# The maxima of the second attention go round three PSUM banks

## The chip, the cores and the metric

The kernel runs on one core of a Trainium2 chip. The metric is the device time of one execution in microseconds (us). Three runs of the kernel before took 4518.84, 4525.36 and 4537.07 us, a median of 4525.36. The profile is of one further execution.

## What is computed

The model is a chain of residual blocks over four sequences of 512 tokens and 128 channels: a gated mixture of experts, a linear attention, the experts again, a six-layer block of local attention and feed-forward (`_L1_ffn_ref`), the attention that this case is about (`_L1_attn_ref`), and the six-layer block once more.

```python
x = x + 0.5 * _L1_ffn_ref(_layernorm(x), ...)
x = x + _L1_attn_ref(_layernorm(x), ...)
x = x + 0.5 * _L1_ffn_ref(_layernorm(x), ...)
```

The second attention has 16 heads of 8 channels and two softmax branches, which share queries and values and differ in their keys:

```python
q, k, v, kp = (_heads(x @ W.T, B, T) for W in (W_Q, W_K, W_V, W_K_prime))
attn   = softmax(einsum('bhqd,bhkd->bhqk', q, k)  / sqrt(8))
attn_p = softmax(einsum('bhqd,bhkd->bhqk', q, kp) / sqrt(8))
out = alpha * (attn @ v) + (1 - alpha) * (attn_p @ v)
return out.transpose(0, 2, 1, 3).reshape(B, T, C) @ W_O.T
```

## The kernel before

The program has four parts, run one after the other: the front (experts and linear attention), the first six-layer block, the second attention (`l1_attn`, line 1061), the second six-layer block. In the six-layer blocks the order of work on every engine is written out by hand. In the second attention only TensorE's order is (`slots`, line 1271, under `manual_schedule` for PE); the order on the vector, scalar and GpSimd engines and on SP's DMA queue is chosen by a scheduler that simulates the program when it is built.

The attention's work is cut into 32 units (`todo`, line 1220): four sequences b, two branches br, four groups hg of four heads. Queries and keys are held as three bfloat16 pieces stacked along the contraction, 72 rows of products and zeros up to row 96; rows 96 to 98 of the keys hold ones and those of the queries take the negated row maxima, in three pieces as well. One matmul then yields score minus maximum.

A unit passes through these steps:

- `max` (line 1145), 16 times: one matmul S (L1147) of 128 queries against 512 keys into a PSUM bank, and one reduction on the vector engine, DVE (L1148), which writes the negated maximum into a column of `nm`.
- `pieces` (L1156 to L1160, GpSimd): the maxima are split into three pieces.
- `rows`: a transpose (nmT, L1165), a copy on ScalarE, ACT (npc, L1167), a DMA to DRAM (nd, L1169) and a DMA back into rows 96 to 98 of the queries (q<-nd, L1170). Both are issued on SP's queue.
- `score` (L1176, L1177), 16 times: the matmul ST, the other way round, into one of four banks with the tag `mm`, and an exponential on ACT.
- `mix` (L1184): E times the values and a column of ones, accumulated in the bank `av`.
- `norm` (L1194 to L1205): a transpose (avT, in an `mm` bank), a reciprocal, a scaling and a multiplication on DVE.

A unit is worked on over four slots. In slot n (`slot`, line 1236) the maxima of unit n, the rows of unit n-1, the scores and mixes of unit n-2 and the last mixes and the normalisation of unit n-3 share the engines. A slot has four blocks (kt = 0 to 3). In each block TensorE's order is S, ST, S, ST, S, ST, S, ST and then the mix of the block before. `rows` comes after the second pair of block 1, `norm` at the end of block 1, so that its transposes open block 2. In slots 0 and 1 there are maxima but no scores; in slots 32 to 34 there are scores but no maxima.

Between the units, in blocks 0 and 3, runs the preparation of the next sequence (`prep`, line 1100): a layer norm and its transpose (yT), three projections (qp, L274 to L276), each split into three pieces by ACT, DVE (L1114), ACT and GpSimd (L1116) and written to DRAM by three DMAs (pd, L1120), and the projection of the values (vp). `load` (line 1094) brings the queries and keys of the next sequence back from DRAM by four DMAs, one for each group of heads (q<-pd and k<-pd, L1098). When a sequence is done, `final` multiplies by W_O (OT, wop) and adds to x (L1217). All these DMAs go through SP's queue, which works in order.

PSUM has eight banks of 512 fp32 values in each partition. The pool (line 63) gives four to the tag `mm`, one to `n2`, two to `S` (its tile has 1024 values, line 69) and one to `av`. A call of `bank` allocates a tile; with one buffer to a tag, the new tile waits until the one before has been released, that is until its last reader is done.

In `max` the maxima alternate between the tags `S` and `n2`: for an even `qt` a new tile of `S` is allocated, of which the first 512 values are used, for an odd one a tile of `n2`. The second bank of `S` is not used in this stage. The six-layer blocks use `S` whole, for their scores, and `n2` for their norms.

Of the kernel before, what the change touches and what calls it, by code (L numbers as in the profile page):

```python
# [66 lines left out]

BANKS = {"mm": 4, "n2": 1, "S": 1, "av": 1}


def bank(g, tag, shape=(128, 512), name=None):
    n = math.prod(shape[1:])
    t = g.psum.tile([128, 1024 if tag == "S" else 512], F32, tag=tag, name=name or tag, bufs=BANKS[tag])[0:shape[0], 0:n]
    if len(shape) > 2:
        d = "abcd"[:len(shape) - 1]
        t = t.rearrange("p (%s) -> p %s" % (" ".join(d), " ".join(d)), **dict(zip(d[1:], shape[2:])))
    return t
# [201 lines left out]
class Unit:  # L279


    def __init__(self, g, l, hf, b):
        self.g, self.l, self.hf, self.b = g, l, hf, b
        self.raw, self.pt, self.v = [None, None], {}, [None, None]
        self.rt = [None, None]
        self.sqs, self.S = {}, {}

# [122 lines left out]
    def score(self, k, h):  # L410
# [3 lines left out]
        if h == 0:  # L414
            self.S[k] = S = bank(g, "S", [128, 2, 512])
            for p in range(4):
                for ab in range(2):
                    rows, q = slice(ab * 64, ab * 64 + 64), slice(p * 32, p * 32 + 32)
                    nc.tensor.matmul(S[q, ab].rearrange("p (a b) -> p a b", b=64) if k else S[q, ab], lhsT=g.msel[rows],
                                     rhs=g.mask1[rows].unsqueeze(1).to_broadcast([64, 8, 64]) if k  # L420
                                     else g.mask0[rows].rearrange("k a b c -> k (a b c)"), start=True, stop=False)
        for w in range(4 * h, 4 * h + 4):
            t0 = (8 * k + w) * 32
            n = 64 if t0 else 32
            for p in range(4):
                for ab in range(2):
                    rows = slice(ab * 64, ab * 64 + 64)
                    nc.tensor.matmul(self.S[k][p * 32:(p + 1) * 32, ab, w * 64 + 64 - n:w * 64 + 64],  # L428
                                     lhsT=self.rt[1][rows, p, t0:t0 + 32], rhs=self.rt[0][rows, p, t0 + 32 - n:t0 + 32],
# [631 lines left out]
def l1_attn(g, w, x, ev, t0=0.0, blk=0, ready=None, memory=()):  # L1061
# [32 lines left out]
    def load(b, i):  # L1094

        t = qs[b % 2] if i == 0 else ks[i - 1]
        for hg in range(4):
            nc.sync.dma_start(t[hg // 2][0:SR, hg % 2], dram[(b, i)][:, :, :, hg].rearrange("a c d h n -> (a c d) h n"))  # L1098

    def prep(b):  # L1100
        y = g.wp.tile([128, 4, 128], F32, tag="wvraw", name="y", bufs=1)
        layernorm(g, x[b], y)
        p = bank(g, "mm", name="yT")
        transpose4(g, p, y)
        xT = g.wp.tile([128, 2, 512], FR, tag="rot", name="xT", bufs=3)
        split(g, xT[:, 0, :], xT[:, 1, :], p)
        yield
        for i, n in enumerate(("W_Q", "W_K", "W_K_prime")):
            p = bank(g, "mm", name="qp")
            mm3(nc, p, W[n][:, 0, :], W[n][:, 1, :], xT[:, 0, :], xT[:, 1, :])  # L1110
            pc = tile_of(g, "pt", [128, 3, 512], BF, "pc")
            t1 = g.wp.tile([128, 512], F32, tag="woraw", name="t1", bufs=1)
            nc.scalar.copy(pc[:, 0, :], p)
            nc.vector.tensor_tensor(t1, p, pc[:, 0, :], ALU.subtract)  # L1114
            nc.scalar.copy(pc[:, 1, :], t1)
            (nc.gpsimd if b else nc.vector).tensor_tensor(pc[:, 2, :], t1, pc[:, 1, :], ALU.subtract)  # L1116
            dram[(b, i)] = d = g.dr.tile([3, 3, 8, 4, 4, 512], BF, tag="pd", name="pd", bufs=4)
            for c in range(3):
                dst = d[:, c] if i == 0 else d[c]
                nc.sync.dma_start(dst.rearrange("j d g h n -> (d g h) j n"), pc)  # L1120
            if i == 0 and b:
                load(b, i)
            yield
        p = bank(g, "mm", [128, 4, 16, 8], "vp")
        for t in range(4):
            ts = slice(t * 128, (t + 1) * 128)
            mm3(nc, p[:, t], xT[:, 0, ts], xT[:, 1, ts], W["W_V"][:, 0, :], W["W_V"][:, 1, :])
        if b == 0:
            vxs.extend(columns())
        vx = vxs[b % 2]  # L1130
        nc.vector.tensor_copy(vx[:, :, 0:144].rearrange("p t (h c) -> p t h c", c=9)[:, :, :, 0:8], p)
        st[b] = tile_of(g, "t2", [128, 4, 16, 8], name="O")
        yield

    class Unit1:
# [7 lines left out]
            self.nm = tile_of(g, "nm", [128, 4, 4], bufs=3)  # L1143

        def max(self, h, qt):
            S = bank(g, ("S", "n2")[qt % 2], name="S")
            nc.tensor.matmul(S, lhsT=self.q[0:R0, h, qt * 128:(qt + 1) * 128], rhs=self.k[0:R0, h, :], start=True, stop=True)  # L1147
            nc.vector.tensor_reduce(self.nm[:, h, qt:qt + 1], S, AX.X, ALU.max, negate=True)  # L1148

# [68 lines left out]
            yield  # L1218

    todo = [(b, br, hg) for b in range(4) for br in range(2) for hg in range(4)]  # L1220
    units = []
    extra = []

    def first():
# [8 lines left out]
    def pick(n):  # L1233
        return units[n] if 0 <= n < len(units) else None

    def slot(n):
        if n < len(todo):
            units.append(Unit1(*todo[n]))
            if n % 8 == 3 and n < 24:
                extra.append(prep(n // 8 + 1))  # L1240

        if n % 8 == 4 + LAG and n < 24:
            load(n // 8 + 1, 1)
        if n % 8 == LAG and 8 < n < 32:
            load(n // 8, 2)
        U, P, A, B = (pick(n - k) for k in (0, 1, LAG, LAG + 1))
        for kt in range(4):
            if (kt in (0, 3) or not A) and extra:
                if next(extra[0], 0) == 0:
                    extra.pop(0)  # L1250
            for h in range(4):
                if U:
                    U.max(kt, h)
                if A:
                    A.score(kt, h)
                if kt == 1 and h == 1 and P:
                    P.rows()
                if h == 3:
                    for c in range(2):
                        if kt and A:  # L1260
                            A.mix(kt - 1, c)
                        if kt == 0 and B:
                            B.mix(3, c)
            if kt == 1 and B:
                B.norm()
                if (B.br, B.hg) == (1, 3):
                    extra.insert(0, B.final())
            if U and kt == 3:
                U.pieces()

    def slots():
        for n in range(len(todo) + LAG + 2):
            with g.tc.manual_schedule(engines={mybir.EngineType.PE}):
                if n < len(todo) + LAG + 1:
                    slot(n)
                else:
                    for e in extra:
                        for _ in e:
                            pass
            yield  # L1280
# [18 lines left out]
def macaron(tc, w, out):  # L1299
    with ExitStack() as ctx:  # L1300
# [13 lines left out]
        def side():  # L1314
# [9 lines left out]
        l1_ffn(g, w, x, ev, xd=xd, ready=names[-4:])  # L1324
        ev.part = 2
        ready = l1_attn(g, w, x, ev, PHASES[0], ready=[((5, b), "fadd", 0) for b in range(4)],
                        memory=[((5, 1, 3), "vproj", 7, 1), ((5, 1, 3), "score", 1, 1, 0)])
        ev.part = 3
# [28 lines left out]
```

## Time and profile before

| | |
|---|---|
| median of three runs | 4525.36 us |
| the profiled execution: its time | 4526.41 us |
| its span, first to last instruction | 4524.2 us |
| busy in the span: PE, DVE, ACT, POOL | 86%, 82%, 58%, 55% |
| mean granted clock of PE | 0.94 |
| first and last reduction of the maxima (L1148) | 2306.5 and 2773.2 us |
| reductions L1148 | 512, 684 ns each |
| exponentials L1177 | 512, 597 ns each |

PE is TensorE's matmuls, PEld its weight loads, DVE the vector engine, ACT ScalarE, POOL GpSimd, and SPq the queue from which SP issues DMAs. Times in a timeline count from the start of the span. A line gives the start, the duration, the engine, the source line, the operation, what it writes and reads, how many instructions were merged into it, and in brackets the idle time before it with the instruction that ended it. Several matmuls overlap in TensorE, so the distance from start to start says more than the duration. The busy shares are means over the whole span; the second attention is about a tenth of it.

### The profile page before, as it was taken

The page shows a single profiled execution, that of the slowest core. Times are in us where ns is not written, and L with a number is a line of the kernel's source. Part 1 is how long each engine was busy: PE and PEld are TensorE (multiplying, and loading weights), DVE is VectorE, ACT ScalarE, POOL GpSimd, SP SyncE. Part 2 cuts the span into 40 slices and gives each one's busy share as a digit, 9 for nine tenths or more (in the row PEclk, how much of TensorE's full clock was granted, in tenths as well). Part 3 has the DMA queues.
Part 4 walks back from the last instruction along what each step waited for, and adds up shares of the span by engine and source line. Part 5 has one row for each costly group of instructions (what it writes and reads, how often), then busy time and mean ns, then how long its engine had stood idle before and what let it go on. Part 6 is the DMA issues. An engine that isn't in the chain of part 4 may idle for free.

```text
span 4524.2 us, 150230 instructions
## 1 busy us (share of the span) xinstructions
PE 3890.1 (86%) x66432; PEld 2671.8 (59%) x66436; DVE 3712.5 (82%) x6415; ACT 2622.0 (58%) x5050; POOL 2491.7 (55%) x2164
## 2 busy tenths in 40 slices
PE   8989978898888888898869998888889888888886
PEld 6666646666666666666523333666666666666654
DVE  6967978888888888988767775888888888888886
ACT  4534455665565565665546666556566556565653
POOL 3625656666666666666410111666666666666663
PEclk8989989999999999999979999999999999999998
DMA  2000033433424334343331221333343333333432
GB/s 61 19 10 15 19 85 74 91 70 80 91 61 91 70 80 90 64 90 73 82 102 35 68 73 35 83 69 81 77 92 70 79 79 75 82 69 79 86 62 48
DMA packets 163852, 312.44 MB, mean 69 GB/s; under 512 B 41304, under 2 KB 125664, under 8 KB 138176
## 3 DMA queue, kind: packets, MB, share of 16 engines
q0 software_dynamic: 31008, 202.40, 22.6%
q1 hardware_dynamic: 132192, 100.44, 7.6%
q8 instruction: 520, 8.52, 0.8%
q14 instruction: 132, 1.08, 0.1%
HBM read 77.49 MB, written 17.69 MB: 21 GB/s over the span
## 4 chain that ended last, share of the span: by engine, by line
DVE 41%; PE 36%; DMA 11%; issue 6%; ACT 3%; POOL 2%; SPq 0%; DVEq 0%; ACTq 0%; POOLq 0%
DMA xs<-x 9%; DVE sm L448 4%; DVE E L440 3%; DVE h L935 3%; PE vps L401 3%; PE S L428 3%; DVE mx L438 3%; DVE xT L269 3%; PE av L1184 3%; PE S L1147 3%; DVE pt L455 3%; DVE rtq L308 3%; PE av L471 2%; PE qkps L274 2%; DVE nm L1148 2%
## 5 line engine op out<-in xcount | busy, mean ns | idle before, releaser
L310 POOL TENSOR_TENSOR raw<-raw,rot 128x512 f32<-128x512 f32 x768 | 1007.1, 1363 | 540.1 <-ACT raw L300 536.5
L300 ACT COPY raw<-qkps 128x512 f32<-128x512 f32 x768 | 453.4, 590 | 654.3 <-PE qkps L276 636.6
L401 PE MATMUL vps<-vo,xF 128*32 128x256 f32 x12288 | 748.3, 386 | 35.6 <-issue 26.3
L401 PEld LDWEIGHTS vps<-vo,xF 128*32 128x32 f32 x12288 | 408.4, 111 | 321.3 <-issue 77.5
L452 POOL TENSOR_TENSOR E<-E,smr 128x1024 f32<-128x1024 f32 x192 | 389.5, 2028 | 310.5 <-DVE smr L450 161.5
L407 ACT COPY vx<-vps 128x512 f32<-128x512 f32 x768 | 426.9, 584 | 105.5 <-PE vps L401 103.3
L303 ACT ACTIVATE sq<-qkps 128x512 f32<-128x512 f32 x768 | 473.0, 616 | 0.0
L443 POOL TENSOR_TENSOR E<-E,rq 128x1024 f32<-128x1024 f32 x192 | 388.9, 2026 | 96.5 <-DVE E L440 57.6
L471 PE MATMUL av<-vx,pt 128*32 128x128 f32 x11904 | 382.0, 275 | 59.4 <-DVE x L478 33.2
L274 PE MATMUL qkps<-xT,wqk 128*128 128x512 f32 x768 | 344.9, 449 | 80.4 <-DVE rtq L308 42.1
L471 PEld LDWEIGHTS av<-vx,pt 128*32 128x32 f32 x11904 | 335.6, 110 | 117.4 <-DVE x L478 50.3
L1148 DVE TENSOR_REDUCE nm<-S 128x1 f32<-128x512 f32 x512 | 326.6, 684 | 81.6 <-PE S L1147 73.8
L308 DVE TENSOR_TENSOR rtq<-qkps,rot 128x512 f32<-128x512 f32 x384 | 259.9, 685 | 135.7 <-ACT sq L303 134.1
L1177 ACT ACTIVATE E<-ST 128x512 f32<-128x512 f32 x512 | 289.5, 597 | 116.3 <-PE ST L1176 105.6
L383 DVE TENSOR_TENSOR rtk<-rtk,R 128x512 f32<-128x512 f32 x384 | 254.1, 672 | 106.1 <-PE R L380 105.6
L677 PE MATMUL fout<-w,ge 128*128 128x128 f32 (+1 forms) x1152 | 229.0, 376 | 121.3 <-DVE rtk L383 118.5
L937 POOL TENSOR_TENSOR h<-r,h 128x512 fp32r<-128x512 f32 x128 | 181.5, 1418 | 258.0 <-DVE h L935 245.1
L275 PE MATMUL qkps<-xT,wqk 128*128 128x512 f32 x768 | 312.5, 407 | 4.9 <-DVE xT L269 2.8
L276 PE MATMUL qkps<-xT,wqk 128*128 128x512 f32 x768 | 310.2, 404 | 6.3 <-issue 6.3
L428 PE MATMUL S<-rtk,rtq 64*32 64x64 f32 (+1 forms) x24576 | 290.3, 229 | 10.5 <-issue 8.5
L428 PEld LDWEIGHTS S<-rtk,rtq 64*32 64x32 f32 x24576 | 283.9, 108 | 26.1 <-issue 13.3
L677 PEld LDWEIGHTS fout<-w,ge 128*128 128x128 f32 (+1 forms) x1152 | 214.8, 285 | 131.6 <-DVE rtk L383 127.5
(257 smaller groups left out, 8822.8 us busy)
## 6 DMA issues: line engine op xcount, KB each, us to landing
rtk<-raw POOLq DMA_DIRECT2D x192, 512.0 KB, 6.8
rtq<-raw POOLq DMA_DIRECT2D x192, 512.0 KB, 6.4
pd<-pc SPq DMA_DIRECT2D x36, 384.0 KB
wqkr<-in_L_ffn_Wqk SPq DMA_DIRECT2D x192, 64.0 KB
rot<-in_c_rot SPq DMA_DIRECT2D x24, 512.0 KB
k<-pd SPq DMA_DIRECT2D x32, 288.0 KB
r<-in_L_ffn_W SPq DMA_DIRECT2D x32, 256.0 KB
wvraw<-in_L_ffn_WvT SPq DMA_DIRECT2D x24, 256.0 KB
```

What stands on the lines that cost most here:

```text
L274: nc.tensor.matmul(out, lhsT=wh, rhs=xh, start=True, stop=False)
L300: nc.scalar.copy(raw, ps)
L303: nc.scalar.activation(sq, ps, AF.Square)
L308: nc.vector.tensor_tensor(self.rt[s][:, i, :], ps, rot[:, 0, :], ALU.mult)
L310: nc.gpsimd.tensor_tensor(raw, raw, rot[:, 1, :], ALU.mult)
L401: nc.tensor.matmul(ps[p * 32:(p + 1) * 32, ww, :], lhsT=xF[:, t0:t0 + 32], rhs=g.vo[(self.l, self.hf, p // 2)][:, p % 2, :], start=True, s ...
L407: nc.scalar.copy(self.v[th][:, 2 * t:2 * t + 2, :], ps)
L428: nc.tensor.matmul(self.S[k][p * 32:(p + 1) * 32, ab, w * 64 + 64 - n:w * 64 + 64], lhsT=self.rt[1][rows, p, t0:t0 + 32], rhs=self.rt[0][r ...
L452: nc.gpsimd.tensor_tensor(E, E, r.unsqueeze(2).to_broadcast([128, 16, 64]), ALU.mult)
L471: g.nc.tensor.matmul(self.av[ww * 32:(ww + 1) * 32, k, :], lhsT=self.pt[w // 8][:, ab, w % 8, role, :], rhs=self.v[src // 8][:, src % 8, a ...
L677: nc.tensor.matmul(self.o[:, t, :], lhsT=h[0:k, t * 128:(t + 1) * 128], rhs=g.F[self.l].w2[0:k, i, :], start=(i == 0 and t == 0), stop=(i ...
L1148: nc.vector.tensor_reduce(self.nm[:, h, qt:qt + 1], S, AX.X, ALU.max, negate=True)
```

## The change

The maxima no longer allocate a bank for each matmul. In slot 0 two tiles are allocated and held for the whole stage: `two`, both banks of `S`, and one bank of `n2`. Their three banks stand in the list `sb`, with the bank of `n2` between the halves of `two`, and the maxima take them in turn. `len(units)` counts the units begun and each has 16 maxima, so the index counts on by one from each maximum to the next, also across slots.

```diff
         def max(self, h, qt):
-            S = bank(g, ("S", "n2")[qt % 2], name="S")
+            S = sb[(16 * len(units) + 4 * h + qt) % 3]
             nc.tensor.matmul(S, lhsT=self.q[0:R0, h, qt * 128:(qt + 1) * 128], rhs=self.k[0:R0, h, :], start=True, stop=True)
             nc.vector.tensor_reduce(self.nm[:, h, qt:qt + 1], S, AX.X, ALU.max, negate=True)
...
-    units = []
+    units, sb = [], []
...
     def slot(n):
+        if n == 0:
+            two = bank(g, "S", [128, 2, 512], "S")
+            sb.extend([two[:, 0], bank(g, "n2", name="S"), two[:, 1]])
         if n < len(todo):
             units.append(Unit1(*todo[n]))
```

No matmul, reduction or DMA is added, removed or moved in TensorE's order. What changes is on which earlier reduction an S waits: the second before it until now, the third before it after the change.

## The prediction

> **What bounds the kernel now.** I began with the stage that the change touches. In the windows view (columns: stretch, length, then busy time of PE, PEld, DVE, ACT, POOL, then granted clock, DMA share, GB/s) the 30 slots in which maxima and scores run together take 446 us:
>
> ```profile
> 2328.14:2774.22 446.08, 414.28 (x3117) 164.89 (x3120) 334.40 (x640) 307.65 (x584) 48.09 (x174) 1.00 0.18 54
> ```
>
> No engine but PE is near full, and PE's clock is 1.00. Next I read the groups of the stage by line:
>
> ```profile
> L1148 DVE TENSOR_REDUCE nm<-S 128x1 f32<-128x512 f32 x512 | 326.6, 684 | 81.6 <-PE S L1147 73.8 <-POOL nc L1158 6.2
> L1147 PE MATMUL S<-k,q 96*128 96x512 bf16 x512 | 202.1, 395 | 51.2 <-DMA k<-pd 18.8 <-DVE nm L1148 18.2 <-issue 0.2
> ```
>
> PE and DVE wait for each other: S for the reduction (18.2 us), the reduction for S (73.8 us). The 18.2 is too small, since a matmul is drawn 0.38 long while the next can start 0.22 after it; starts tell more. So, third, the timeline of one block, PE and DVE:
>
> ```profile
> 2522.02 0.39 PE L1147 MATMUL S<-k,q 96*128 96x512 bf16 x1
> 2522.24 0.38 PE L1176 MATMUL ST<-q,k 128*128 128x512 bf16 x1
> 2522.44 2.49 DVE L1148 TENSOR_REDUCE nm<-S 128x1 f32<-128x512 f32 x4 [0.61 <-PE S L1147]
> 2522.46 0.38 PE L1147 MATMUL S<-k,q 96*128 96x512 bf16 x1
> 2522.68 0.38 PE L1176 MATMUL ST<-q,k 128*128 128x512 bf16 x1
> ...
> 2523.19 0.38 PE L1147 MATMUL S<-k,q 96*128 96x512 bf16 x1
> ...
> 2523.41 0.38 PE L1176 MATMUL ST<-q,k 128*128 128x512 bf16 x1
> 2523.79 0.38 PE L1147 MATMUL S<-k,q 96*128 96x512 bf16 x1
> ...
> 2524.00 0.38 PE L1176 MATMUL ST<-q,k 128*128 128x512 bf16 x1
> 2524.31 1.07 PE L1184 MATMUL av<-E,vx 128*32 128x256 f32 x16
> ```
>
> Unhindered, PE starts every 0.22 us. The third S starts 0.51 after the ST before it, the fourth 0.38: both banks are full and it waits for a reduction. Here DVE has only started 0.42 after the block's first S, because PE spent the 1.0 us before on the mix. Loss per such block: 0.29 + 0.16 = 0.45 us of 3.30. So PE's order sets the end, and its stalls are two-bank stalls.
>
> **What goes away.** The change adds and removes no instruction; S waits for the reduction three back, not two. I listed, from PE's starts over slots 2 to 31, every S that starts more than 0.22 after an ST. By kind of block: 39 with nothing else, 18.5 us (0.46 typical, some 0.52); 29 with the transpose of the maxima (nmT), 5.6; 29 with the normalisation (avT), 19.1 (0.59 each); 9 with a projection (qp), 9.7 (1.05 or 1.12); 6 with a transpose of y or O, 5.2; 3 with wop, 2.5; 3 with vp, 0.9; the start of slot 2, 1.0. Sum 62.4 us.
>
> Is the third bank enough? A bank is reused 0.75 after the start of the reduction that empties it (2522.44 to 2523.19). The fourth S would wait for the first reduction: 0.42 + 0.75 = 1.17 after the block's start, and it is due at 6 x 0.22 = 1.32, so it does not wait. In a normalisation block the first reduction starts 0.9 late, behind the reciprocal: free at 1.66, due at 0.49 + 1.32 = 1.81. In a projection block only the first reduction lies ahead of the subtraction (L1114): free 1.17 after the first S, due at 1.32. Then a plain slot falls from 13.88 to 13.88 - 0.46 - 0.17 - 0.59 - 0.46 = 12.2 us. DVE fits: 16 reductions, 0.60 from start to start ((2.49 - 0.69) / 3), and 0.8 for the normalisation make 10.4. ACT too: 16 exponentials at 0.55 at most (2.19 for four) and 0.8 of copies make 9.6.
>
> **What stays or comes back.** (a) The 1.0 us at slot 2's start is at half clock and stays. (b) Around each of the three output projections DVE runs almost unbroken (2461.4 to 2472.8); I keep 0.8 us of the 2.9 there, and 0.2 in each of three y blocks: 3.0. (c) Three times the stage is held by DMA, and there earlier matmuls gain nothing. SP's queue, second time:
>
> ```profile
> 2492.59 1.50 SPq L1120 DMA_DIRECT2D pd<-pc  x3
> 2497.37 1.55 SPq L1098 DMA_DIRECT2D q<-pd  x4
> 2499.02 0.97 SPq L1120 DMA_DIRECT2D pd<-pc  x2
> ...
> 2500.73 0.95 SPq L1169 DMA_DIRECT2D nd<-npc  x1
> 2508.25 0.31 SPq L1098 DMA_DIRECT2D k<-pd  x1
> 2508.98 0.24 SPq L1170 DMA_DIRECT2D q<-nd  x1
> ```
>
> ```profile
> 2511.89 0.39 PE L1176 MATMUL ST<-q,k 128*128 128x512 bf16 x1 [0.57 <-DMA q<-nd]
> ```
>
> The projection at 2488.15 starts pd; q<-pd waits for it to land, pd of the next projection (1.15 MB) follows, the maxima's rows (nd) queue behind that, k<-pd waits for pd, and only then goes q<-nd, for which the slot's first ST waits, with the mixes and all maxima after it on PE. That chain is 23.7 us from its projection and holds no two-bank wait. PE's stalls inside it (1.05 + 1.12 + 0.17 + 0.59 + 1.05 + 0.30 = 4.28) turn into waiting for q<-nd: 3 x 4.28 = 12.8 us come back. (d) These waits become 0.6 + 4.3 = 4.9 us of idle PE. Elsewhere the trace shows what follows such a gap:
>
> ```profile
> 3110.60:3114.90 4.30, 0.04 (x4) 0.02 (x1) 2.17 (x11) 0.60 (x4) 0.80 (x2) 0.85 0.41 117
> 3114.90:3120.40 5.50, 5.50 (x25) 3.10 (x26) 4.64 (x9) 4.07 (x9) 4.59 (x5) 0.50 0.01 3
> ```
>
> 5.5 us at half clock: 2.7 us of matmuls lost. Bounds: nothing, if the waits come out short, to 3 x 2.7 = 8; I take 7.5, since the gap here is the longer one. (e) In four ordinary slots q<-nd is issued late (2385.07, 2454.19, 2547.82, 2727.29), 2.1 to 2.5 us before its ST; that margin shrinks by 1.05 (normalisation and a plain block). The loaded case above took 2.9 to land, so 0 to 1.9 each; I take 0.6: 2.4 us. (f) A gain: in slots 0 and 1, maxima alone, two take 1.367 us (2306.52 to 2307.89), 0.683 each; without the round trip DVE can go at 0.60: 32 x 0.08 = 2.6.
>
> The sum: 62.4 - 1.0 - 3.0 - 12.8 - 7.5 - 2.4 + 2.6 = 38.3 us. The profiled span of 4524.2 becomes 4485.9. Around it the run has 2.2 us more (4526.41), and the median of the runs is 4525.36, so on that footing 4487.
>
> The row says that the small stalls cost no clock: 1.00 over 446 us with a stall in nearly every block. The Trainium skill ("TensorE: Matmul & The Clock Gate", section "A second HAM failure mode: psum-queue depth-cycling") holds that short PE idles from cycling PSUM banks make the clock swing between half and full; by it part of the stage would now be cold and a third bank would also win clock, an estimated 22 us for each tenth of 446 us at half clock. By the row this is zero, and I go by the row.
>
> **The rivals.** *The DMA waits do not bind.* If nd is issued ahead of the second pd, because the rows are ready 2.2 us sooner, (c) and (d) fall away: 4487 - 20.3 = 4467. Against it: SP takes pd as soon as it is ready, and q<-pd, pd and nd together move over 2.3 MB between 2497.4 and 2508.7, whose transfers nd shares.
>
> *The wait moves to the score banks.* ST, nmT, avT and qp share four banks. In a normalisation block, if the fourth ST takes avT's bank, it waits until L1201 has read it, 2.6 after the block's start, just when that ST starts today (2520.70 for a block from 2518.10): the 0.59 in 29 blocks, 17 us, would stay: 4504. Against it: a bank emptied by an exponential is free earlier, and PE waited 1.1 us in all for one.
>
> *Slower: the held pair counts as one tile.* Two of the three banks are halves of one tile. If a write to one half must wait for the reader of the other, the half that follows its sister waits for the reduction just before it: 0.42 + 0.75 = 1.17 after the last S in place of 0.44, 0.73 lost. It decides as soon as it holds at all: of 160 such S in slots 2 to 31, a quarter open a block, behind the mix, and lose nothing; 120 x 0.73 = 88, the other half's 160 waits at today's mean (62.4 / 480) 21, slots 0 and 1 another 5: 114 against 62.4 removed, so 4525 + 52 = 4577. Against it: loads of k into halves of one SBUF tile are issued a slot apart (2389.68, 2403.49), each released by the last reader of its own half.
>
> **How the numbers follow.** The forecast has 0.62, with its own range 4475 to 4500 from (d) and (e); no DMA wait 0.17; score banks 0.12; held pair 0.06; 0.03 for the unforeseen. A difference under 0.5%, 22.6 us, can't be told from no change: the line lies at 4502.7. Faster: 0.62 + 0.17 + a quarter of the score banks = 0.82; slower 0.07; the rest 0.11. The range runs from below the DMA rival to above the score-bank one, 4460 to 4510.
>
> **What would show it.** Right: plain blocks of 2.85 us, normalisation 3.33, projection 3.65; L1147 waiting for L1148 near nothing; three waits of 4 to 5 us on q<-nd with a clock under 1.00 after each; the stage about 38 us shorter and the rest unchanged. Wrong: S waiting for the reduction just before it; ST waiting for L1201; other orders on SP or DVE than now, which would move the three DMA waits.

## The result, and the profile after

The change makes the kernel slower. Four runs after have a median of 4583.18 us (4580.06 to 4593.67), four runs before (the three above and one more) 4522.49 us: a ratio of 1.0132, interval 1.0104 to 1.016. The forecast was 4487, and its range ended at 4510.

The profiled execution after has a span of 4589.9 us, 65.7 more than before. From the first reduction of the maxima (L1148) to the last, the stage takes 532.0 us (2310.1 to 2842.1) where it took 466.6: 65.4 of the 65.7 are there. The windows view of the kernel after, slots 2 to 31 (columns as in the prediction: stretch, length, busy PE, PEld, DVE, ACT, POOL, granted clock, DMA share, GB/s):

```profile
2338.79:2843.00 504.21, 411.42 (x3117) 165.59 (x3120) 344.94 (x639) 305.40 (x584) 48.12 (x173) 0.99 0.16 48
```

The same 3117 matmuls, with busy times that differ by at most 11 us on any engine, are spread over 504 us in place of 446. The clock is not the cause: it is at one half until 2348.2 us, at the start of slot 2, and at 1.00 from there to the end of the stage. So the engines wait more. The groups of the kernel after by line, and then a row of the view of waits (engine, line and what it waited for: us in total, times, longest), first of the kernel before and then of the kernel after:

```profile
L1148 DVE TENSOR_REDUCE nm<-S 128x1 f32<-128x512 f32 x512 | 334.1, 686 | 136.6 <-PE S L1147 133.8 <-POOL nc L1158 1.8
L1147 PE MATMUL S<-k,q 96*128 96x512 bf16 x512 | 201.2, 397 | 124.2 <-DVE nm L1148 97.7 <-DMA k<-pd 19.4 <-issue 0.2
```

```profile
PE S L1147 <- DVE nm L1148: 18.2, 51, 0.9
```

```profile
PE S L1147 <- DVE nm L1148: 97.7, 150, 1.6
```

PE's wait for the reduction was 18.2 us in 51 waits and is 97.7 in 150; DVE's for S was 73.8 and is 133.8. Each waits for the other more, which is how a chain of two engines without a buffer between them looks. The timeline shows on which reduction S now waits. One normalisation block of the kernel after, PE and then DVE:

```profile
2553.97 0.38 PE L1147 MATMUL S<-k,q 96*128 96x512 bf16 x1
2554.19 0.38 PE L1176 MATMUL ST<-q,k 128*128 128x512 bf16 x1
2555.13 0.38 PE L1147 MATMUL S<-k,q 96*128 96x512 bf16 x1 [0.56 <-DVE nm L1148]
2555.35 0.38 PE L1176 MATMUL ST<-q,k 128*128 128x512 bf16 x1
2555.57 0.38 PE L1147 MATMUL S<-k,q 96*128 96x512 bf16 x1
2555.78 0.38 PE L1176 MATMUL ST<-q,k 128*128 128x512 bf16 x1
2556.29 0.38 PE L1147 MATMUL S<-k,q 96*128 96x512 bf16 x1
```

```profile
2554.39 0.69 DVE L1148 TENSOR_REDUCE nm<-S 128x1 f32<-128x512 f32 x1
...
2555.55 1.29 DVE L1148 TENSOR_REDUCE nm<-S 128x1 f32<-128x512 f32 x2
```

The second S starts at 2555.13, just after the reduction of the first one ends (2554.39 + 0.69 = 2555.08): a wait for the reduction **one** back, 1.16 after the S before it. The third starts 0.22 after the ST, without a wait. The fourth starts at 2556.29, when the reduction of the second has ended (2555.55 + 0.69): **two** back. None waits three back. This is one turn of the three banks: the four S shown write the second half of the held pair, the first half, the bank of `n2`, and again the second half. The second half must wait for the reader of the first, the first half, which follows its sister directly, for the reader of the second, and `n2`, which comes next, needs nothing that the first half has not waited for already. The waits in the built program say the same: of 170 S in the first half 164 wait for the reduction one back, of 171 in the second half 164 wait for the one two back, and 165 of the 171 in `n2` need no wait of their own. (All but one of the others stand at six slot ends, where the next slot's first S, one in `n2`, was moved ahead of the last ST and the mix.)

Summed over slots 2 to 31 as in the prediction (starts more than 0.22 after an ST), by the bank that S writes:

```
                        first half   n2    second half   sum (us)
before, by index mod 3      20.4    22.2      19.8        62.4
after                       93.1     0.7      20.6       114.4
```

(Before, the columns only sort by the same count; there the banks were two.) All 109 S of the first half that follow an ST stall, 0.85 us each on average. Since a slot has 16 maxima, the turn of three moves on by one place from slot to slot, but four S of the first half stand inside the blocks of every slot; one that opens a block hardly loses, since the mix covers its wait. The plain slots 23, 24 and 25, from first reduction to first reduction, take 14.40, 17.12 and 15.96 us, 47.5 together, against 13.88, 13.81 and 13.81, 41.5 together, before. Slot 23 looks short and slot 24 long because the first S of slot 24 is one of those that stand ahead of the last ST and the mix of the slot before.

### The profile page after: what moved, and what is told of

Read it like the earlier page. It is cut to its first block, busy times and chain, and to the rows that moved or that the text cites. A ratio compares the mean times of both kernels' runs of the same rounds, so it can differ in the third digit from the quotient of the medians.

```text
span 4589.9 us, 150229 instructions
## 1 busy us (share of the span) xinstructions
PE 3887.1 (85%) x66432; PEld 2670.3 (58%) x66436; DVE 3718.3 (81%) x6415; ACT 2621.2 (57%) x5050; POOL 2494.6 (54%) x2164
## 4 chain that ended last, share of the span: by engine, by line
DVE 41%; PE 36%; DMA 11%; issue 6%; ACT 3%; POOL 2%; SPq 0%; DVEq 0%; ACTq 0%; POOLq 0%
DMA xs<-x 10%; DVE nm L1148 4%; PE vps L401 4%; DVE sm L448 3%; DVE h L935 3%; PE S L428 3%; DVE E L440 3%; DVE mx L438 3%; DVE xT L269 3%; PE av L471 3%; PE av L1184 3%; DVE pt L455 2%; DVE rtq L308 2%; PE S L1147 2%; PE qkps L274 2%
## 5 line engine op out<-in xcount | busy, mean ns | idle before, releaser
L1148 DVE TENSOR_REDUCE nm<-S 128x1 f32<-128x512 f32 x512 | 334.1, 686 | 136.6 <-PE S L1147 133.8
L1147 PE MATMUL S<-k,q 96*128 96x512 bf16 x512 | 201.2, 397 | 124.2 <-DVE nm L1148 97.7
```

## The experiments

Two theories were to be told apart. **Theory:** the two halves of the held pair are ordered as one tile, so that a write to one waits for the reader of the other. **Rival:** holding the banks, or the order of work that comes of it, costs the time, and the pair as such is innocent.

**The halves set free.** The kernel after, with the ordering of S behind the two reductions that read other banks declared needless; banks and instructions stay.

```diff
+            m = nc.tensor.matmul(S, ...)
+            reds.append(nc.vector.tensor_reduce(self.nm[:, h, qt:qt + 1], S, ...))
+            if len(reds) > 3:
+                for r in reds[-4:-1][1:]:
+                    g.tc.declare_no_dep(m.ins, r.ins, reason="another bank")
```

> The change, with the waits between the two halves of the held pair declared away: each S waits for the reduction three back and for none nearer. Theory 1 (the loss is the wait of one half on the reader of the other): the two-bank stalls go too, so the forecast of the prediction holds after all, 4487 us with 4467 to 4504 around it, and three waits of 4 to 5 us on q<-nd appear. Rival (holding the banks for the whole stage makes the scheduler order the other engines worse, and that costs the time): it stays near 4580.

Measured: 4476.24 us (4466.45 to 4485.12), ratio 0.9904, interval 0.9876 to 0.9932. Each S now waits for the reduction three back, and the time is 107 us below the kernel after. (The scheduler, which simulates the program, puts a few instructions elsewhere: 18 of the 37,684 places in PE's order and 19 of the 628 DMAs on SP's queue hold another one. The 18 are the six exchanges at slot ends; without them PE's order is that of the kernel before.) The stalls of the list sum to 4.1 us. A plain block of this kernel, PE and DVE (the lines behind the edit are three higher, ST is L1179):

```profile
2526.53 0.39 PE L1147 MATMUL S<-k,q 96*128 96x512 bf16 x1
...
2526.98 0.38 PE L1147 MATMUL S<-k,q 96*128 96x512 bf16 x1
2527.20 0.38 PE L1179 MATMUL ST<-q,k 128*128 128x512 bf16 x1
2527.42 0.38 PE L1147 MATMUL S<-k,q 96*128 96x512 bf16 x1
2527.63 0.38 PE L1179 MATMUL ST<-q,k 128*128 128x512 bf16 x1
2527.85 0.38 PE L1147 MATMUL S<-k,q 96*128 96x512 bf16 x1
...
2529.38 0.39 PE L1147 MATMUL S<-k,q 96*128 96x512 bf16 x1
```

```profile
2527.03 2.49 DVE L1148 TENSOR_REDUCE nm<-S 128x1 f32<-128x512 f32 x4 [0.44 <-PE S L1147]
```

Every start is 0.22 after the last, DVE runs its four reductions unbroken, and the block takes 2.85 us (2526.53 to 2529.38). PE writes one half while DVE reads the other with no loss that the starts show: the order was kept by the program's waits, not by the banks.

**Three separate tiles.** The kernel after, with three tiles of one bank each, the third taken from `mm`.

```diff
-            two = bank(g, "S", [128, 2, 512], "S")
-            sb.extend([two[:, 0], bank(g, "n2", name="S"), two[:, 1]])
+            sb.extend([bank(g, "S", name="S"), bank(g, "n2", name="S"), bank(g, "mm", name="S")])
```

> The three banks are three tiles: one S, one n2, and one of the four mm banks held through the stage, so ST, nmT, avT and qp have three. Theory 1: no S waits for a reduction nearer than three back; what is gained on S is partly lost on ST, which finds avT's bank or an exponential in the way in the normalisation block (0.3 to 0.6 us in 29 blocks, 9 to 17 us): 4490 to 4515. Rival (holding is what costs): near 4580.

Measured: 4484.08 us, ratio 0.9926, interval 0.9904 to 0.9949. Three banks held through the stage are fast when no two are of one tile, with nothing declared. The stage is 433.8 us long, 12.4 more than with the halves free (421.4): a plain slot takes 12.37 us against 12.00. The starts place it: the normalisation block takes 3.57 against 3.34, and in the block of nmT, which takes 3.09 against 2.96, the second ST starts 0.30 after its S instead of 0.22 (2526.43 and 2526.13). That fits scores that are short of a bank, with three `mm` banks for ST, nmT, avT and qp; which wait it is, is not shown.

**Two separate tiles, held.** The kernel after, with one bank of `S` and one of `n2` held and taken in turn.

```diff
-            S = sb[(16 * len(units) + 4 * h + qt) % 3]
+            S = sb[qt % 2]
...
-            two = bank(g, "S", [128, 2, 512], "S")
-            sb.extend([two[:, 0], bank(g, "n2", name="S"), two[:, 1]])
+            sb.extend([bank(g, "S", name="S"), bank(g, "n2", name="S")])
```

> Two banks held through the stage, one S and one n2, taken in turn as before: holding without a pair. Theory 1: the same waits two back as before, so the time of before, 4522 within 0.5%. Rival (holding is what costs): clearly slower, toward 4580.

Measured: 4519.67 us, ratio 0.9996, interval 0.9982 to 1.001, stage 466.5 us. Holding costs nothing: the rival falls.

**The pair alone.** The two halves in turn, without `n2`.

```diff
-            S = sb[(16 * len(units) + 4 * h + qt) % 3]
+            S = sb[qt % 2]
...
-            sb.extend([two[:, 0], bank(g, "n2", name="S"), two[:, 1]])
+            sb.extend([two[:, 0], two[:, 1]])
```

> Only the held pair, its two halves in turn, n2 left out: each S should wait for the reduction just before it. Theory 1: an S can start no sooner than 1.17 us after the last, so a plain block is 3 x 1.17 + 0.22 + 0.31 + 1.0 = 5.0 us where it was 3.3; some 120 blocks and the 32 maxima of slots 0 and 1 make 4700 to 4750. Rival (holding is what costs, halves are independent): two banks in turn as before, between 4522 and 4580.

Measured: 4786.15 us in one run, stage 744.5 us. Like the kernel just shown it uses two banks, halves of one tile here and two tiles there, and it is 266 us slower. Part of a block of this kernel, PE, and two of its windows:

```profile
2602.57 0.38 PE L1147 MATMUL S<-k,q 96*128 96x512 bf16 x1 [0.56 <-DVE nm L1148]
...
2603.77 0.38 PE L1147 MATMUL S<-k,q 96*128 96x512 bf16 x1 [0.60 <-DVE nm L1148]
...
2604.93 0.59 PE L1147 MATMUL S<-k,q 96*128 96x512 bf16 x1 [0.56 <-DVE nm L1148]
2605.31 0.63 PE L1176 MATMUL ST<-q,k 128*128 128x512 bf16 x1
```

```profile
2450.00:2550.00 100.00, 70.97 (x447) 24.52 (x440) 51.63 (x86) 45.21 (x81) 6.00 (x24) 0.89 0.05 14
2750.00:2850.00 100.00, 72.98 (x424) 27.13 (x417) 49.73 (x87) 44.85 (x81) 7.66 (x23) 0.85 0.20 64
```

S now follows S at 1.2 us, with 0.56 to 0.60 of idle PE each time, and the granted clock of the stage falls to between 0.80 and 0.95; the last S shown is the first of a stretch at half clock (0.59 and 0.63 long). The time above the expectation goes with these stretches; how much of it they hold was not measured.

**Three banks in a turn of four.** First half, `n2`, second half, `n2`: all three banks are in use, and the halves stand two places apart.

```diff
-            S = sb[(16 * len(units) + 4 * h + qt) % 3]
+            S = sb[qt]
...
-            sb.extend([two[:, 0], bank(g, "n2", name="S"), two[:, 1]])
+            n2 = bank(g, "n2", name="S")
+            sb.extend([two[:, 0], n2, two[:, 1], n2])
```

> The three held banks are taken in a turn of four: first half of the pair, bank of n2, second half, bank of n2. All three banks are in use, but an S in a half follows its sister half at a distance of two, and n2 comes round at a distance of two. If the pair counts as one tile, every S waits for the reduction two back, as in the kernel before: the stalls stay at 62 us and the time at 4521 (4512 to 4532), a ratio of 1.000. If the halves are independent, an S in a half waits for the reduction four back, half of the stalls go and the time falls to about 4495.

Measured: 4516.07 us, ratio 0.9993, interval 0.9977 to 1.0009, stalls of 62.7 us. The view of waits of this kernel has the row of the kernel before with its times and sums but for 0.1 us:

```profile
PE S L1147 <- DVE nm L1148: 18.3, 51, 0.9
```

What decides is how far back a bank's *tile* was last used, not how many banks are in the turn.

**One `mm` bank held in the kernel before.** The control for the three separate tiles: two matmuls that the computation does not need, one in the first maximum and one in the last, keep an `mm` bank through the stage.

```diff
+            if (len(units), h, qt) in ((1, 0, 0), (len(todo), 3, 3)):
+                if not held:
+                    held.append(bank(g, "mm", name="held"))
+                nc.tensor.matmul(held[0], ...)
```

> The kernel before, with one of the four mm banks held through the stage (two extra matmuls use it, one at its start and one at its end), so that ST, nmT, avT and the projections share three. It is the control for the kernel with three separate tiles, which was 8 us above the one with the halves set free (4484 against 4476). If the held mm bank costs that, this one comes out near 4529, 8 above the kernel before, with ST waiting for the exponential or for L1201. If the 8 us were chance or came from the order of the work, it stays at 4521.

Measured: 4520.4 us, ratio 1.0002, interval 0.9986 to 1.0018, stage 466.4 us. It costs nothing that shows here, where S stalls in nearly every block; the 12.4 us of the three separate tiles stand beside it where those stalls are gone.

**The rows on another queue, and the halves free once more.** With the halves free three waits are left. The view of PE's waits in the stage, and SP's queue around the second of them, both of the first kernel with the halves free:

```profile
PE ST L1179 <- DMA q<-nd: 12.8, 3, 4.7
```

```profile
2486.28 2.05 SPq L1098 DMA_DIRECT2D q<-pd  x4
2488.38 0.38 SPq L1120 DMA_DIRECT2D pd<-pc  x1
2488.81 0.68 SPq L1172 DMA_DIRECT2D nd<-npc  x1
2496.11 0.30 SPq L1098 DMA_DIRECT2D k<-pd  x1
2496.45 0.28 SPq L1173 DMA_DIRECT2D q<-nd  x1
```

q<-nd goes out 7.6 us after nd, behind k<-pd, and the ST that needs it starts at 2499.90. The windows of the same kernel around it show what the wait does to the clock:

```profile
2494.50:2499.20 4.70, 1.25 (x11) 0.95 (x9) 1.41 (x3) 0.00 (x0) 1.66 (x6) 0.99 0.51 134
2499.20:2506.00 6.80, 6.10 (x26) 1.92 (x27) 2.56 (x4) 3.04 (x6) 0.00 (x0) 0.50 0.82 262
```

6.8 us at half clock follow, from 2499.2 here and from 2376.3 and 2608.4 at the other two. The next kernel issues nd and q<-nd from GpSimd:

```diff
-            nc.sync.dma_start(d, pc)
-            nc.sync.dma_start(self.q[R0:KR], ...)
+            nc.gpsimd.dma_start(d, pc)
+            nc.gpsimd.dma_start(self.q[R0:KR], ...)
```

> The kernel with the halves set free, with the two DMAs of the maxima's rows (nd and q<-nd) issued from GpSimd's queue instead of SP's. With the halves free three waits of ST for q<-nd were left, 4.3 to 5 us each, 13 in all, each followed by 6.8 us at half clock, that is 3.4 us lost each. Theory: the waits come from SP's queue, where nd stands behind pd and q<-nd behind k<-pd. Then both go: 13 + 10 = 23 us less some for a slower issue, 4476 falls to 4456 (4450 to 4465). Rival: the transfers of q<-pd and pd themselves hold nd up, or the rows are late on any queue: the three waits stay and the time is 4476. Second rival: GpSimd's issue of a DMA is slower than SP's, q<-nd comes late in ordinary slots too, 30 waits of a microsecond or so: 4490 or more.

> The kernel with the halves set free once more, beside the three others: 4476 (4466 to 4486), a ratio of 0.990, with three waits for q<-nd of 4 to 5 us.

Measured: 4467.08 us (4458.07 to 4475.4), ratio 0.9885, interval 0.9862 to 0.9908, and 4477.63 us, ratio 0.9904, interval 0.9882 to 0.9927, for the kernel with the halves free. The medians differ by 10.5 us, half of what was expected. With four runs each their ranges overlap (the second kernel ran from 4471.75 to 4482.35), but the profiled stage is 410.9 us long in place of 421.8. From slot to slot:

```
first reduction to first reduction, us   slot 5   14      22      6      23
halves free (second run)                 18.85   18.80   19.04   12.06  12.07
rows issued from GpSimd                  11.92   16.91   12.29   14.40  13.23
before                                   14.29   14.01   14.55   13.88  13.88
```

The waits are shorter and not gone: PE waits for q<-nd 5.8 us in all, at most 2.2 at a time, against 14.7 in the second run with the halves free. The row of slot 6 holds what is left of slot 5's wait, that of slot 23 what is left of slot 22's, and neither is followed by half clock; the one in slot 14 is. The GpSimd queue in slot 14 shows what is left of the chain:

```profile
2476.74 0.56 POOL L1172 DMA_DIRECT2D nd<-npc  x1 [1.11 <-ACT npc L1170]
2482.71 0.51 POOL L1173 DMA_DIRECT2D q<-nd  x1 [5.40 <-DMA nd<-npc]
```

nd goes out when its rows are ready, and then takes 5.7 us to land; in a stretch without the big transfers it takes 1.7. While it is under way, so are the four q<-pd issued from 2476.71 on and a pd. So SP's order was one part of these waits. That the load on the transfers is the other is read from what was under way at the time; no run took the load away. The theory and the first rival of the expectation held in part. The second rival falls: plain slots without a wait take 11.9 to 12.1 us, as with SP. This version has the lowest median of those that were run.

## Why the prediction was wrong

**The step that failed** is the first sentence of "What goes away": "S waits for the reduction three back, not two". "The change" says the same ahead of it. It was read off the three names in `sb`, and it holds for none of the S. One of the three waits one back, one two back, one not at all. All that was built on it, 62.4 us removed, fell with it. That nothing moves in TensorE's order was not quite right either: at six slot ends the next S now stands ahead of the last ST and the mix.

**The rival that came true** had the mechanism and nearly the size. Its 4577 stands beside a median of 4583. It put the stalls of slots 2 to 31 at 88 + 21 = 109 us, and the list has 114.4. Inside the first term two errors partly cancelled: 120 S of the first half at 0.73 were expected to lose 88, and 109 at 0.85 lost 93. A quarter of the 160 do open a block, but 10 more follow an nmT and not an ST, and so are not in the list; and normalisation and projection blocks lose more than plain ones. The second half was put at 21 and lost 20.6. Slots 0 and 1 were given 5 and grew by 7.4. The span grew by 65.7 and not 52: slots 0 and 1 grew by 7.4 and slots 2 to 31 by 58.0, of which 52.0 are in the list, some 4 are S that follow an nmT, which the list leaves out, and 2 were not placed.

**Why it had only 0.06.** The evidence against it was loads of k into halves of one SBUF tile, each released by its own half's reader. The two loads it names go into two tiles: by the order of `load`, the one at 2389.68 fills the second half of one tile and the one at 2403.49 the first half of the next. The second half of that one is loaded at 2417.37, 13.9 us later, so the reading holds, with other lines. It says nothing here all the same: it is about a DMA into SBUF, and the waits of a matmul into PSUM turned out otherwise. No row of the profile before showed a matmul into one half of a PSUM tile while the other half was being read, since the stage used only the first 512 values of `S`. For an ordering that no row shows, a price of +52 us and a chance of 0.06 did not go together with a range that ended at 4510. Why the two kinds of tile differ stays open; no run asked it.

**The rest of the forecast**, on the premise that failed, can be read from the kernel with the halves free, 4476 and 4478 us in two medians against 4487:

- Blocks: plain 2.85 us, normalisation 3.34, projection 3.66; forecast 2.85, 3.33 and 3.65. The arithmetic of three banks was right; DVE and ACT keep up, and a plain slot takes 12.0 us where 12.2 was forecast. The other 0.2 is a term that the list of 62.4 left out: before, the S behind each nmT also waited, 0.18 us in 30 slots, 5.2 in all, and with the halves free it starts 0.11 after the nmT, without a wait.
- Stalls that stay, (a) and (b): 4.0 us forecast, and the list of the new kernel sums to 4.1, but that is luck. About 0.7 of it is the start of slot 2, where 1.0 was forecast, and 1.2 lies at the output projections and y blocks, where 3.0 was forecast. The other 2.2 are starts at half clock behind the three waits for q<-nd.
- (c) and (d): three waits for q<-nd of 12.8 us in all, where three of 4.9 were forecast, each followed by half clock, for 6.8 us where 5.5 had been read from the trace.
- (e): forecast 2.4 us of late q<-nd in ordinary slots; PE waits for q<-nd three times and no more, so this is nought.
- (f): forecast 2.6 us from slots 0 and 1; together they are 1.95 shorter (19.91 to 19.92 against 21.86).
- In sum the stage is 45 us shorter (466.6 to 421.4 and 421.8), where 38.3 was forecast. The difference is the 5.2 us behind the nmT and some 2 of stalls that went, less 0.7 in (f); so what came back through the DMA waits and their clock is the forecast 22.7 us in sum, though not term by term.

The rival in which the DMA waits do not bind (4467) was wrong as it stood: they bind. The one in which the wait moves to the score banks (4504) is nought with four `mm` banks and shows, as 12 us, with three.

## What to carry to other kernels

Count the banks of a rotation by the tiles they belong to: two banks cut from one tile may be ordered as one, and a rotation is then as deep as the distance to the sister's last reader, however many banks are in it. Where a wait can be read from the built program or from one block of a timeline, look at which earlier instruction it names before pricing what it saves. A row about another memory or another engine is no evidence on an ordering; when none of the right kind exists, both outcomes belong in the range.

## What the hardware showed that was not expected

Short stalls do cost clock when there are enough of them. With a stall in nearly every block (before) slots 2 to 31 ran at 1.00, and so they did after the change, from 2348.2 us on, with 97.7 us of waits in the stage (their 0.99 comes from the start of slot 2 alone). With 0.56 to 0.60 of idle PE behind nearly every S (the pair alone, one run) the clock fell to 0.80 to 0.95. The section of the Trainium skill that the prediction weighed ("TensorE: Matmul & The Clock Gate", "A second HAM failure mode: psum-queue depth-cycling") tells of such swings from short idles between groups of matmuls; the prediction's row was right for this kernel, and the run with the pair alone shows the behaviour that the page describes.

A long wait brought the same time at half clock in each case: 6.8 us at 0.50 with 3.4 to 5.4 us of waiting, nine times in nine (three waits each in both runs with the halves free and with three separate tiles). At 2.2 us it went both ways: in the kernel with the rows on GpSimd's queue the ST at 2488.38, after 2.20 us of waiting, ran at half clock (0.61 long), and the one at 2382.87, after 2.16, at full clock (0.39).
